# Strassen's seven products for an adjacency multiplication, laid between the products of the weights (Trainium2, float32, one core)

## The chip, the cores and the metric

The kernel runs on one core of a Trainium2 chip. The metric is the device time of one execution in microseconds, of the slowest core; here there is only one. A core has a matrix engine (TensorE, PE in the profile, with its weight loads as PEld), VectorE (DVE), ScalarE (ACT), GpSimd (POOL) and SyncE (SP), which in this kernel only issues transfers. Each engine works through its own stream of instructions in the order in which the program wrote them, and instructions of different engines are tied by waits.

## What is computed

Input `x` is 64 batches of 256 tokens by 512 features, all float32. Two residual layers follow one another; only the first is touched.

```python
# --- layer 0 (adj_preln) ---
h = jnp.maximum(_layernorm(x, axis=-1), 0.0)      # no gain or bias
y = jnp.einsum('nm,bmd->bnd', adj, h)             # adj is 256 x 256, one for all batches
x = x + jnp.einsum('bnd,do->bno', y, weight) + bias
# --- layer 1: layer norm, relu, attention with 8 heads, output product, residual ---
```

## The kernel before

**Groups.** The 64 batches are taken two at a time (`GB = 2`), so there are 32 groups (`NG`). Layer 0 goes through all groups, and leaves two things in DRAM: the new residual and the normed, relued and transposed input of layer 1. Layer 1 then goes through the groups again. Around the border the two are mixed a little: the queries, keys and values of group 0 are made around the weight products of group 31.

**Layer 0 of one group (`layer0`, L702).** First the adjacency product: for each of four feature chunks of 128, and for each batch, two 128x256 matmuls (one for each half of the 256 input tokens) gather into one PSUM bank, 16 matmuls in all (L714), and ScalarE copies each full bank to `yT` (L724). Then the product with the 512x512 weight. It is made by `project` (L456) with Strassen's algorithm in Winograd's form: both operands are cut into 2x2 blocks, some sums of blocks are made beforehand, and seven products take the place of eight. Each product is four 128x256 matmuls (`product`, L448). The seven are seven steps, here called S0 to S6: a11·b11, a12·b21, s2·t2, s3·t3, s1·t1, a22·t4, s4·b22. They accumulate in two long-lived PSUM banks and one short one, and after each of them VectorE adds the bank to a quarter of `x` (L665). The sums t1 to t4 of `yT` are made on GpSimd (L446, `Halves.sums`); those of the weight are made once.

**Layer norms.** `ready` (L678) makes the norm ahead of the adjacency product for a group that is two ahead: for each of four token tiles a statistics instruction and an aggregation on VectorE (L42, L43, "moments"), scale and shift on VectorE and GpSimd (`norm_scales`, L51 to L54), and a relu with that scale and shift on ScalarE (L693). `finished` (L758) makes the norm ahead of layer 1: statistics of each finished quarter of `x` on VectorE (L761, L766), the same scale and shift, a relu on ScalarE (L741), and a 32x32 block transpose on VectorE (`turn`, L747).

**Transfers.** All are issued by SyncE in order: `load` (L295, eight transfers for one group's `x`), `leave_residual` (L751, four for each batch), `leave_hidden` (L756, four for the group).

**What sets the order.** A counter of steps: `run` takes one step of a generator and then calls `tick`, and `after(n, f)` puts `f` at the n-th tick from now. So each engine's order is written out by the program through these delays, and nothing is moved later. A group before has 11 steps (four of the adjacency, seven of the weight); `wait` in `finished` is the number of steps to the relu. Eight PSUM banks are handed out by `bank` and returned by `give`; four buffers of `x` and two of `h` go round.

Of the kernel before, what the change touches and what calls it, by code (L numbers as in the profile page):

```python
# [198 lines left out]
def kernel(  # L199
# [48 lines left out]
    def bank(shape, name, seed=None):  # L248

        i = next(i for i in free_banks if seed is None or whole[i])  # L250
        free_banks.remove(i)
        t = psum.tile(shape, F32, tag=f"bank{i}", name=name)
        bank_of[id(t)] = (i, t)
        if seed is not None:
            nc.scalar.copy(t, seed[:, None, :].to_broadcast(shape))
        return t
# [14 lines left out]
    def tick():  # L271
        clock[0] += 1
        due = sorted((e for e in later if e[0] <= clock[0]), key=lambda e: e[:2])
        later[:] = [e for e in later if e[0] > clock[0]]
        for _, _, fn, args in due:
            fn(*args)
# [14 lines left out]
    def load(g):  # L291
        X[g] = xpool.tile([P, T, D], F32, tag="x", name=f"x_{g}")
        for k in range(GB):
            for i in range(NI):
                nc.sync.dma_start(blocks_of(X[g], i, k), by_block(x[g * GB + k], i))  # L295
# [27 lines left out]
    def turn_adjacency():  # L323
        adj_p = tmp.tile([P, NT, N], F32, tag="u", name="adj_p")
        for u in range(NT):
            nc.vector.tensor_copy(adj_p[:, u, :].rearrange("p (t i b) -> p i t b", i=NI, t=NT),
                                  adj_r[:, u, :].rearrange("p (i t b) -> p i t b", i=NI, t=NT))
        pa = bank([P, NT, N], "pa")
        for t in range(NT):
            for u in range(NT):  # L330
                nc.tensor.transpose(pa[:, t, u * P:(u + 1) * P],
                                    adj_p[:, u, t * P:(t + 1) * P], ident)
        nc.vector.tensor_copy(adjT, pa)  # L333
        give(pa, False)
# [329 lines left out]
    def add(o, ps, u):  # L664
        nc.vector.tensor_tensor(o, ps, u, op=ALU.add)  # L665
# [4 lines left out]
    def split_bias(row):  # L670

        nc.vector.tensor_tensor(row[:, HF:], row[:, HF:], row[:, :HF], op=ALU.subtract)

    def seeded(row, name):
        return tuple(bank([P, 2, N], f"{name}{b}", seed=row[:, h * HF:(h + 1) * HF]) for h, b in enumerate("ac"))


    def ready(g, moments_at, scales_at, relus_at, batches=1):  # L678


        xt = X[g]
        mv = small.tile([P, T, 2], F32, tag="mv", name=f"mv0_{g}")
        n = T // batches
        h = []

        def scales(i):
            h.append(norm_scales(nc, small, mhalf, mv[:, i * n:(i + 1) * n, :], f"0_{g}_{i}"))
            if i == 0:
                H0[g] = act.tile([P, T, D], F32, tag="h", name=f"h_{g}", bufs=2)

        def relu(t):
            rs, nb = h[t // n]
            nc.scalar.activation(H0[g][:, t, :], xt[:, t, :], AF.Relu,  # L693
                                 bias=nb[:, t % n:t % n + 1], scale=rs[:, t % n:t % n + 1])

        for t in range(T):
            after(moments_at[t], moments, nc, small, mv, t, xt[:, t, :], f"0_{g}")
            if (t + 1) % n == 0:
                after(scales_at[t // n], scales, t // n)
            after(relus_at[t], relu, t)  # L700

    def layer0(g):  # L702

        xt, h = X.pop(g), H0.pop(g)

        yT = act.tile([P, DC, GN], F32, tag=f"yT{g % 2}", name=f"yT_{g}")
        halves = Halves(f"y_{g}", [yT[:, :, k * N:(k + 1) * N] for k in range(GB)], g % 2 if g < NG - 1 else 0)
        pss = {}

        def adjacency(d, b):  # L710
            if d not in pss:
                pss[d] = bank([P, GN], f"py_{g}_{d}")
            for k in range(NT):
                nc.tensor.matmul(pss[d][:, b * N:(b + 1) * N], h[:, b * NT + k, d * P:(d + 1) * P],  # L714
                                 adjT[:, k, :], start=(b + k == 0), stop=(k == NT - 1), skip_group_check=True)

        if g == 0:
            for d in range(DC):
                adjacency(d, 0)
        for d in range(DC):  # L720
            for b in range(1 if g == 0 else 0, GB):
                adjacency(d, b)
            ps = pss.pop(d)
            nc.scalar.copy(yT[:, d, :], ps)  # L724
            give(ps)
            halves.sums(nc.gpsimd, ("t1",) if d < 2 else ("t2",), d % 2)
            if d == 3:
                halves.sums(nc.gpsimd, ("t3", "t4"))
            if d == 2:
                seeds = seeded(b0_r, f"w_{g}")  # L730
            yield

        mv = small.tile([P, T, 2], F32, tag="mv", name=f"mv1_{g}")
        st = [small.tile([P, 2, nc.vector.BN_STATS_DIM], F32, tag="st1", name=f"st1_{g}_{t}", bufs=8) for t in range(T)]
        h1 = act.tile([P, T, D], F32, tag="h1", name=f"h1_{g}")
        r = act.tile([P, DC * NI, GB, NT, 32], F32, tag="r", name=f"r_{g}")
        done = []

        def relu(k, rs, nb):
            for t in range(NT):  # L740
                nc.scalar.activation(h1[:, k * NT + t, :], xt[:, k * NT + t, :], AF.Relu,  # L741
                                     bias=nb[:, t:t + 1], scale=rs[:, t:t + 1])

        def turn(k):

            for t in range(NT):
                nc.vector.transpose(r[:, :, k, t, :], h1[:, k * NT + t, :].rearrange("p (j b) -> p j b", b=32))  # L747

        def leave_residual(k):
            for i in range(NI):  # L750
                nc.sync.dma_start(by_block(X1[g][k], i), blocks_of(xt, i, k))  # L751

        def leave_hidden():
            dst = HT[g].rearrange("(j f) d i k n -> i f d j (k n)", f=32)
            for i in range(NI):
                nc.sync.dma_start(dst[i], r[32 * i:32 * i + 32].rearrange("p (d j) k t b -> p d j (k t b)", j=NI))  # L756

        def finished(i, k):  # L758
            o = quarter(xt, i, k)
            for t in range(NT):  # L760
                nc.vector.bn_stats(st[k * NT + t][:, i, :], o[:, t, :])  # L761
            done.append(k)
            if done.count(k) == 2:
                s = slice(k * NT, (k + 1) * NT)
                for t in range(k * NT, (k + 1) * NT):
                    nc.vector.bn_aggr(mv[:, t, :], st[t])  # L766
                rs, nb = norm_scales(nc, small, mhalf, mv[:, s, :], f"1_{g}_{k}")
                wait = 2 if g < NG - 1 else 3
                after(wait, relu, k, rs, nb)
                after(1 if len(done) < 4 else 2, leave_residual, k)  # L770
                after(wait + 1, turn, k)
                if len(done) == 4:
                    after(wait + 2, leave_hidden)

        yield from project(W["0"], halves, True, f"w_{g}", lambda i, k: quarter(xt, i, k), add_to, finished, seeds)


# [12 lines left out]
    def hidden_sums(g, *steps):  # L790

        HH[g] = Halves(f"h_{g}", [H1T[g][:, k] for k in range(GB)], 0 if g else 1)
        for step, n in zip(steps, ("t3", "t1", "t2", "t4")):
            after(step, HH[g].sums, nc.gpsimd, (n,))
# [188 lines left out]
    def run(gen, steps=99):  # L983

        for _ in zip(range(steps), gen):
            tick()
# [1 line left out]

    side = [[] for _ in range(NG)]
    mask_steps, bias_steps = masks(), out_bias()  # L990
    STEPS = 11
    for i, n in enumerate("qkvo"):
        side[2 + 2 * i].append((load_layer1, n))
        side[4 + 4 * i].append((lambda n: weight_sums(nc.gpsimd, L1[n][0], n, [2 + STEPS * j for j in range(4)]), n))
# [4 lines left out]

    ready(0, (0, 0, 2, 2), (0, 2), (1, 1, 3, 3), batches=2)  # L1000
    load(1)
    tick()
    turn_adjacency()
    split_bias(b0_r)
    tick()
    weight_sums(nc.vector, w0_sb, "0", (0, 0, 6, 7))
    load(2)
    tick()
    tick()
    for g in range(NG):  # L1010
        for fn, *args in side[g]:
            fn(*args)

        if g == 0:
            ready(1, (1, 2, 3, 4), (5,), (6, 7, 8, 9))
            ready(2, (8, 8, 10, 11), (12,), (16, 17, 18, 19))
        elif g + 2 < NG:
            ready(g + 2, (1, 4, 7, 8), (9,), (16, 17, 18, 19))
        if g == NG - 2:
            hidden_sums(0, 1, 2, 12, 16)  # L1020
        steps = layer0(g)
        run(steps, 4)
        if g + 3 < NG:
            load(g + 3)
        if g == NG - 3:
            load_hidden(0)
        if g == NG - 1:
            load_hidden(1)
            break
        run(steps)  # L1030
    run(queries_keys(0))
    score(0, 0, 12)
    tick()
    run(steps)
    hidden_sums(1, 1, 2, 6, 7)
# [80 lines left out]
```

## Time and profile before

The median of three runs is 2672.7 us (2672.06 to 2672.92). The profiled execution spans 2669.9 us, with a mean TensorE clock of 0.999.

| what | where in the profile | figure |
|---|---|---|
| adjacency matmuls, 128x256 | L714 on PE, 1024 records | 227.8 us busy |
| their weight loads | L714 on PEld, 1024 records | 195.4 us busy |
| first adjacency matmul, first weight product of group 0 | timeline | 12.07 us, 21.02 us |
| end of group 31's adjacency product, where layer 1's first product begins | timeline | 614.88 us |
| t sums of `yT` on GpSimd | L446, two rows of 96 | 88.0 and 87.2 us busy |
| relu ahead of the adjacency product | L693 on ACT, 128 | 93.9 us, 805 ns each |
| relu ahead of layer 1 | L741 on ACT, 128 | 97.1 us, 807 ns each |
| statistics of finished quarters | L761 on DVE, 256 | 96.4 us, 418 ns each |

A float32 matmul has two records in the profile, as has its weight load. A row of a group reads: line, engine, operation, output and input, shapes, count, then busy time, mean of one, and the idle time of that engine before it with what ended it. A row of the timeline reads: start, busy time, engine, line, operation, output and input, shapes, count of merged records, and in brackets the idle time of the engine before it and the releaser. Ends of matmuls are modelled, so the step from one product's start to the next one's is the measure of its cost.

### The profile page before, as it was taken

How to read it: one execution, taken by the hardware profiler on the slowest of the kernel's cores; microseconds unless marked ns; L12 is line 12 of the kernel's file. 1: busy time of each engine (PE TensorE's matmuls, PEld its weight loads, DVE VectorE, ACT ScalarE, POOL GpSimd, SP SyncE). 2: the span in 40 equal slices, each digit the busy share in tenths (PEclk: the TensorE clock that was granted, in tenths of full speed). 3: DMA queues.
4: the chain of work that ended last, by engine and by line, in shares of the span. 5: the costliest groups of instructions: out<-in, count | busy, mean ns of one | idle time of the engine just before them, and what ended most of it. 6: DMA issues, size and time to landing. Idle time of an engine off the chain costs nothing. (4 is left out here: it accounts for less than half of the span.)

```text
span 2669.9 us, 50186 instructions
## 1 busy us (share of the span) xinstructions
PE 2640.4 (99%) x19332; PEld 2275.8 (85%) x19332; DVE 1849.0 (69%) x4089; ACT 965.3 (36%) x1875; POOL 1793.3 (67%) x1582
## 2 busy tenths in 40 slices
PE   8999999999999999999999999999999999999997
PEld 7888888888888888888888888888888888888885
DVE  6777777774466766666767767667677676676676
ACT  4444445453333333333333333333333333333332
POOL 4454544454787777777777777777777777777775
PEclk9999999999999999999999999999999999999999
DMA  7776666663122211111111111111222111111110
GB/s 185 186 199 169 155 169 166 169 164 78 44 61 58 63 51 48 48 48 48 49 48 48 48 48 48 49 48 49 64 65 62 49 49 48 48 48 49 48 49 33
DMA packets 281059, 210.94 MB, mean 79 GB/s; under 512 B 145904, under 2 KB 212976, under 8 KB 280816
## 3 DMA queue, kind: packets, MB, share of 16 engines
q1 hardware_dynamic: 280352, 207.15, 30.0%
q8 instruction: 155, 2.54, 0.4%
q14 instruction: 88, 0.72, 0.1%
q10 hardware_dynamic: 464, 0.52, 0.1%
HBM read 106.96 MB, written 100.66 MB: 78 GB/s over the span
## 5 line engine op out<-in xcount | busy, mean ns | idle before, releaser
L910 POOL TENSOR_TENSOR a<-a,top 128x1024 f32<-128x1024 f32 x254 | 592.1, 2364 | 488.8 <-DVE a L904 488.8
L904 DVE SCALAR_TENSOR_TENSOR a<-sc,maskT 128x512 f32<-128x512 f32 x512 | 312.1, 682 | 122.0 <-PE sc L898 122.0
L922 POOL TENSOR_TENSOR as<-a 128x512 f32<-128x512 f32 x256 | 318.6, 1277 | 4.0 <-ACT a L915 3.0
L915 ACT ACTIVATE a<-a 128x1024 f32<-128x1024 f32 x256 | 270.9, 1058 | 11.6 <-POOL a L910 10.3
L53 POOL TENSOR_TENSOR rs<-rs,mhalf 128x2 f32<-128x2 f32 (+1 forms) x97 | 78.4, 808 | 268.3 <-DVE nb L52 268.2
L951 DVE RECIPROCAL rest<-rest 128x128 f32<-128x128 f32 x256 | 224.6, 921 | 37.6 <-ACT rest L947 37.6
L898 PE MATMUL sc<-q,k 64*128 64x256 f32 x2048 | 238.4, 382 | 0.0
L938 PE MATMUL pav<-a,v 128*32 128x256 f32 x4096 | 234.0, 379 | 0.0
L898 PEld LDWEIGHTS sc<-q,k 64*128 64x128 f32 x2048 | 194.2, 187 | 44.7 <-issue 26.3
L714 PE MATMUL py<-adjT,h 128*128 128x256 f32 x1024 | 227.8, 381 | 0.9 <-DVE adjT L333 0.9
L714 PEld LDWEIGHTS py<-adjT,h 128*128 128x128 f32 x1024 | 195.4, 191 | 28.4 <-ACT h L693 1.2
L938 PEld LDWEIGHTS pav<-a,v 128*32 128x32 f32 x4096 | 133.5, 110 | 87.9
L741 ACT ACTIVATE h<-x,nb,rs 128x512 f32<-128x512 f32 x128 | 97.1, 807 | 307.2 <-POOL nb L54 307.2
L947 ACT ACTIVATE rest<-pden 128x512 f32<-128x512 f32 x64 | 38.2, 597 | 418.2 <-PE pden L931 418.2
L665 DVE TENSOR_TENSOR k<-k,k 128x128 f32<-128x128 f32 (+1 forms) x300 | 96.1, 353 | 126.1 <-PE k L564 124.0
L446 POOL TENSOR_TENSOR t_y<-yT 128x256 f32<-128x256 f32 (+1 forms) x96 | 88.0, 917 | 44.5 <-ACT yT L724 41.2
L665 DVE TENSOR_TENSOR x<-o,x 128x128 f32<-128x128 f32 (+1 forms) x360 | 111.2, 350 | 3.1
L665 DVE TENSOR_TENSOR q<-q,q 128x128 f32<-128x128 f32 (+1 forms) x300 | 96.1, 353 | 13.8 <-PE q L564 11.7
L665 DVE TENSOR_TENSOR v<-v,v 128x128 f32<-128x128 f32 (+1 forms) x300 | 95.5, 352 | 14.4 <-PE v L564 11.4
L761 DVE BATCH_NORM_STATS2 st<-x 128x6 f32<-128x256 f32 x256 | 96.4, 418 | 4.4
L693 ACT ACTIVATE h<-x,nb,rs 128x512 f32<-128x512 f32 x128 | 93.9, 805 | 10.2 <-POOL nb L54 10.2
L446 POOL TENSOR_TENSOR t_y<-yT,t_y 128x256 f32<-128x256 f32 (+1 forms) x96 | 87.2, 916 | 13.1 <-ACT yT L724 13.0
(4275 smaller groups left out, 6491.5 us busy)
## 6 DMA issues: line engine op xcount, KB each, us to landing
x<-in_x_dram SPq DMA_DIRECT2D x256, 128.0 KB, 3.4
residual<-x SPq DMA_DIRECT2D x256, 128.0 KB, 2.3
hidden<-r SPq DMA_DIRECT2D x128, 256.0 KB, 4.8
h1T<-hidden SPq DMA_DIRECT2D x64, 512.0 KB, 9.6
x<-residual SPq DMA_DIRECT2D x32, 1024.0 KB, 7.5
out_dram<-x SPq DMA_DIRECT2D x62, 512.0 KB, 3.9
w_sb<-in_L_gnn_weight_dram SPq DMA_DIRECT2D x1, 1024.0 KB, 7.3
wq_sb<-in_L_gnn_Wq_dram SPq DMA_DIRECT2D x1, 1024.0 KB, 7.8
```

The costliest lines, as they stand in the source:

```text
L446: eng.tensor_tensor(self.t[n][:, c, :], self.operand(p, c), self.operand(q, c), op=ALU.subtract)
L665: nc.vector.tensor_tensor(o, ps, u, op=ALU.add)
L714: nc.tensor.matmul(pss[d][:, b * N:(b + 1) * N], h[:, b * NT + k, d * P:(d + 1) * P], adjT[:, k, :], start=(b + k == 0), stop=(k == NT - 1 ...
L741: nc.scalar.activation(h1[:, k * NT + t, :], xt[:, k * NT + t, :], AF.Relu, bias=nb[:, t:t + 1], scale=rs[:, t:t + 1])
L761: nc.vector.bn_stats(st[k * NT + t][:, i, :], o[:, t, :])
L898: nc.tensor.matmul(ps[j][:, kt * N:(kt + 1) * N], k[j * HD:(j + 1) * HD, c, kt * P:(kt + 1) * P], q[j * HD:(j + 1) * HD, c, :], start=(kt ...
L904: nc.vector.scalar_tensor_tensor(a[:, j * NT:(j + 1) * NT, :].rearrange("p k n -> p (k n)"), ps[j], SCALE, maskT_f, op0=ALU.mult, op1=ALU.add)
L910: nc.gpsimd.tensor_tensor(a, a, top_b, op=ALU.subtract)
L915: nc.scalar.activation(a, a, AF.Exp)
L922: nc.gpsimd.tensor_tensor(AS[c, b], a4[:, :, 0, :], a4[:, :, 1, :], op=ALU.add)
L938: nc.tensor.matmul(po[f][h * 32:(h + 1) * 32, b * N:(b + 1) * N], v[:, k, h * HD + f * 32:h * HD + f * 32 + 32], A[h // 2, b][:, (h % 2) * ...
L951: nc.vector.reciprocal(rden[:, c * P:(c + 1) * P], den[:, c * P:(c + 1) * P])
```

## The change

The adjacency product of a group is also made by Strassen's algorithm. It isn't a stage of its own any more: its seven products, of four 128x128 matmuls each, are laid between the weight products of the group ahead. The sums that it needs are made on GpSimd: four of adjacency blocks once (`adjacency_sums`, L734), four of the features of each group (`feature_sums`, L745), which follow the relus of that group. The results are put together in `yT` by ScalarE copies and VectorE adds out of PSUM (`adjacency`, L756). Group 0 keeps the old form (`first_adjacency`, L710). Since a group now has seven steps, the delays are set anew: moments, scale and relu of a group are spread over the steps of two groups, and the feature sums over the next. Lines of the changed kernel are given where the text speaks of them.

```diff
-        if g == 0:
-            for d in range(DC):
-                adjacency(d, 0)
         for d in range(DC):
-            for b in range(1 if g == 0 else 0, GB):
-                adjacency(d, b)
...
+    def adjacency_sums():
...
+        for o, p, q in (("t1", block(1, 2), block(1, 1)), ("t2", block(2, 2), AT["t1"]),
+                        ("t3", block(2, 2), block(1, 2)), ("t4", block(2, 1), AT["t2"])):
+            nc.gpsimd.tensor_tensor(AT[o], p, q, op=ALU.subtract)
+
+    def feature_sums(g):
...
+        s1, s2, s4 = (act.tile([P, GB, HF], F32, tag=f"{n}{g % 2}", name=f"{n}_hs_{g}") for n in ("q0", "q1", "k0"))
+        HS[g] = dict(a11=block(1, 1), a12=block(1, 2), a22=block(2, 2), s1=s1, s2=s2, s3=block(2, 1), s4=s4)
+        for o, p, q, op in ((s1, block(2, 1), block(2, 2), ALU.add), (s2, s1, block(1, 1), ALU.subtract),
+                            (block(2, 1), block(1, 1), block(2, 1), ALU.subtract), (s4, block(1, 2), s2, ALU.subtract)):
+            nc.gpsimd.tensor_tensor(o, p, q, op=op)
+
+    def adjacency(g):
...
+        def product(ps, a, b, start=True):
+            for c in range(2):
+                for m in range(GB):
+                    nc.tensor.matmul(ps[:, c, m, :], HS[g][a][:, m, c * P:(c + 1) * P], AT[b],
+                                     start=(start and c + m == 0), stop=True, skip_group_check=True)
...
+        pa = new("a")
+        product(pa, "a11", "b11")
+        nc.scalar.copy(place(0, 0), pa)
+        yield
+        pc = new("c")
+        product(pc, "s3", "t3")
+        nc.scalar.copy(place(1, 1), pc)
+        yield
+        product(pa, "s2", "t2", False)
+        nc.scalar.copy(place(1, 0), pa)
+        yield
+        pb = new("b")
+        product(pb, "a12", "b21")
+        more(pb, 0, 0)
+        give(pb)
+        yield
+        product(pa, "s1", "t1", False)
+        more(pa, 1, 1)
+        yield
+        product(pc, "a22", "t4", False)
+        more(pc, 1, 0)
+        give(pc)
+        yield
+        product(pa, "s4", "b22", False)
+        nc.scalar.copy(place(0, 1), pa)
+        give(pa)
+        after(1, YH[g].sums, nc.gpsimd, ("t1", "t2"))
+        after(3, YH[g].sums, nc.gpsimd, ("t3", "t4"))
+        yield
...
-                wait = 2 if g < NG - 1 else 3
+                wait = 3
...
-    STEPS = 11
+    STEPS = 7
...
     load(1)
+    ready(1, (4, 4, 4, 4), (4,), (5, 5, 6, 6))
+    after(6, feature_sums, 1)
...
-    for g in range(NG):
+    for g in range(NG - 1):
...
-        if g == 0:
-            ready(1, (1, 2, 3, 4), (5,), (6, 7, 8, 9))
-            ready(2, (8, 8, 10, 11), (12,), (16, 17, 18, 19))
-        elif g + 2 < NG:
-            ready(g + 2, (1, 4, 7, 8), (9,), (16, 17, 18, 19))
-        if g == NG - 2:
-            hidden_sums(0, 1, 2, 12, 16)
-        steps = layer0(g)
-        run(steps, 4)
-        if g + 3 < NG:
-            load(g + 3)
+        weighted, turned = layer0(g, seeds), adjacency(g + 1)
+        for i, n in enumerate((0, 0, 0, 1, 1, 2, 3) if g == 0 else (1, 1, 2, 2, 1, 0, 0)):
+            next(weighted)
+            for _ in range(n):
+                next(turned)
+            if i == 5:
+                seeds = seeded(b0_r, f"w_{g + 1}")
+            tick()
+            if i == 3 and g + 3 < NG:
+                load(g + 3)
+
+                ready(g + 3, (2, 2, 3, 3), (3,), (4, 4, 5, 5))
+                after(5, feature_sums, g + 3)
...
+    hidden_sums(0, 1, 1, 2, 2)
+    steps = layer0(NG - 1, seeds)
+    run(steps, 4)
     run(queries_keys(0))
-    score(0, 0, 12)
+    score(0, 0, 6)
```

More of the change, by code (lines that the diff above doesn't have):

```diff
@@ L700, in ready, with begin_y, first_adjacency, part @@
             after(relus_at[t], relu, t)
[L702 to L707, printed above, removed]
+    Y, YH, HS, AT = {}, {}, {}, {}
+    def begin_y(g):
+        yT = Y[g] = act.tile([P, DC, GN], F32, tag=f"yT{g % 2}", name=f"yT_{g}")
+        YH[g] = Halves(f"y_{g}", [yT[:, :, k * N:(k + 1) * N] for k in range(GB)], (g + 1) % 2)
+        return yT
+    def first_adjacency():
+        yT, h = begin_y(0), H0.pop(0)
         pss = {}
-        def adjacency(d, b):
+        def part(d, b):
             if d not in pss:
-                pss[d] = bank([P, GN], f"py_{g}_{d}")
+                pss[d] = bank([P, GN], f"py_{d}")
             for k in range(NT):
@@ L715, in adjacency @@
                                  adjT[:, k, :], start=(b + k == 0), stop=(k == NT - 1), skip_group_check=True)
-        if g == 0:
-            for d in range(DC):
-                adjacency(d, 0)
         for d in range(DC):
-            for b in range(1 if g == 0 else 0, GB):
-                adjacency(d, b)
+            part(d, 0)
+        for d in range(DC):
+            part(d, 1)
             ps = pss.pop(d)
@@ L725, in layer0, with block @@
             give(ps)
-            halves.sums(nc.gpsimd, ("t1",) if d < 2 else ("t2",), d % 2)
+            YH[0].sums(nc.gpsimd, ("t1",) if d < 2 else ("t2",), d % 2)
             if d == 3:
-                halves.sums(nc.gpsimd, ("t3", "t4"))
-            if d == 2:
-                seeds = seeded(b0_r, f"w_{g}")
+                YH[0].sums(nc.gpsimd, ("t3", "t4"))
             yield
+    def adjacency_sums():
+        def block(j, k):
+            return adjT[:, j - 1, (k - 1) * P:k * P]
+        t = act.tile([P, 4, P], F32, tag="t24o", name="adjT_t")
+        AT.update(b11=block(1, 1), b21=block(2, 1), b22=block(2, 2), t1=t[:, 0, :], t2=t[:, 1, :], t3=t[:, 2, :],
+                  t4=t[:, 3, :])
+        for o, p, q in (("t1", block(1, 2), block(1, 1)), ("t2", block(2, 2), AT["t1"]),
+                        ("t3", block(2, 2), block(1, 2)), ("t4", block(2, 1), AT["t2"])):
+            nc.gpsimd.tensor_tensor(AT[o], p, q, op=ALU.subtract)
@@ new lines, in feature_sums, with block @@
+    def feature_sums(g):
+        def block(i, j):
+            return H0[g].rearrange("p (b j) d -> p b j d", b=GB)[:, :, j - 1, (i - 1) * HF:i * HF]
+        s1, s2, s4 = (act.tile([P, GB, HF], F32, tag=f"{n}{g % 2}", name=f"{n}_hs_{g}") for n in ("q0", "q1", "k0"))
[3 more added lines that the diff above has]
+            nc.gpsimd.tensor_tensor(o, p, q, op=op)
@@ new lines, in adjacency, with place, new, more @@
+    def adjacency(g):
+        yT = begin_y(g)
+        H0.pop(g)
+        def place(i, k):
+            return yT[:, 2 * i:2 * i + 2, :].rearrange("p c (b k n) -> p c b k n", b=GB, k=NT)[:, :, :, k, :]
+        def product(ps, a, b, start=True):
[3 more added lines that the diff above has]
+                                     start=(start and c + m == 0), stop=True, skip_group_check=True)
+        def new(n):
+            return bank([P, 2, GB, P], f"py_{g}{n}")
+        def more(ps, i, k):
+            o = place(i, k)
+            add(o, ps, o)
+        pa = new("a")
[27 more added lines that the diff above has]
+        yield
@@ L733, in layer0 @@
+    def layer0(g, seeds):
+        xt, halves = X.pop(g), YH.pop(g)
         mv = small.tile([P, T, 2], F32, tag="mv", name=f"mv1_{g}")
@@ L1001 @@
     load(1)
+    ready(1, (4, 4, 4, 4), (4,), (5, 5, 6, 6))
+    after(6, feature_sums, 1)
     tick()
     turn_adjacency()
+    adjacency_sums()
     split_bias(b0_r)
@@ L1009 @@
     tick()
-    for g in range(NG):
+    steps = first_adjacency()
+    run(steps, 3)
+    seeds = seeded(b0_r, "w_0")
+    run(steps)
+    for g in range(NG - 1):
         for fn, *args in side[g]:
@@ L1014 @@
         if g == 0:
-            ready(1, (1, 2, 3, 4), (5,), (6, 7, 8, 9))
-            ready(2, (8, 8, 10, 11), (12,), (16, 17, 18, 19))
-        elif g + 2 < NG:
-            ready(g + 2, (1, 4, 7, 8), (9,), (16, 17, 18, 19))
-        if g == NG - 2:
-            hidden_sums(0, 1, 2, 12, 16)
-        steps = layer0(g)
-        run(steps, 4)
-        if g + 3 < NG:
-            load(g + 3)
+            ready(2, (1, 1, 2, 2), (2,), (3, 3, 4, 4))
+            after(5, feature_sums, 2)
+        weighted, turned = layer0(g, seeds), adjacency(g + 1)
[10 more added lines that the diff above has]
+                after(5, feature_sums, g + 3)
+        for rest in (weighted, turned):
+            for _ in rest:
+                pass
         if g == NG - 3:
             load_hidden(0)
[L1027 to L1030, printed above, removed]
+    load_hidden(1)
+    hidden_sums(0, 1, 1, 2, 2)
+    steps = layer0(NG - 1, seeds)
+    run(steps, 4)
     run(queries_keys(0))
-    score(0, 0, 12)
+    score(0, 0, 6)
     tick()
```

## The prediction

> **What bounds the kernel now.** I read the page's busy shares first, then the busy time in the stretch of one layer-0 group, then the timeline of that group engine by engine. The page has
>
> ```profile
> PE 2640.4 (99%) x19332; PEld 2275.8 (85%) x19332; DVE 1849.0 (69%) x4089; ACT 965.3 (36%) x1875; POOL 1793.3 (67%) x1582
> ```
>
> so TensorE is the bound overall, and one group of layer 0 (from one adjacency product's start to the next one's; columns after the length: busy PE, PEld, DVE, ACT, POOL) shows no gap on it:
>
> ```profile
> 109.86:128.85 18.99, 18.99 (x89) 16.72 (x88) 14.43 (x39) 8.86 (x14) 9.50 (x13) 1.00 0.65 167
> ```
>
> The timeline around that group's end gives every duration that I need:
>
> ```profile
> 115.71 3.83 SPq L756 DMA_DIRECT2D hidden<-r  x4
> 117.45 2.93 ACT L693 ACTIVATE h<-x,nb,rs 128x512 f32<-128x512 f32 x4
> 119.72 5.34 SPq L295 DMA_DIRECT2D x<-in_x_dram  x8
> 125.40 1.89 PE L453 MATMUL w_5c<-w_sb,t_y 128*128 128x256 f32 x8
> 127.13 1.89 PE L453 MATMUL w_5a<-w_s,yT 128*128 128x256 f32 x8
> 127.23 1.01 POOL L53 TENSOR_TENSOR rs<-rs,mhalf 128x4 f32<-128x4 f32 x1 [6.00 <-DVE nb L52]
> 127.33 0.69 DVE L665 TENSOR_TENSOR x<-w_5c,x 128x512 f32<-128x512 f32 x1
> 128.05 0.75 DVE L761 BATCH_NORM_STATS2 st<-x 128x6 f32<-128x256 f32 x2
> 128.31 0.20 POOL L54 TENSOR_TENSOR nb<-nb,rs 128x4 f32<-128x4 f32 x1
> 128.72 0.33 DVE L766 BATCH_NORM_AGGREGATE mv<-st 128x2 f32<-128x12 f32 x2
> 128.85 7.07 PE L714 MATMUL py<-adjT,h 128*128 128x256 f32 x32
> 129.30 0.68 DVE L665 TENSOR_TENSOR x<-w_5a,x 128x512 f32<-128x512 f32 x1
> 130.41 1.52 ACT L741 ACTIVATE h<-x,nb,rs 128x512 f32<-128x512 f32 x2 [10.03 <-POOL nb L54]
> 131.39 1.31 DVE L747 STREAM_TRANSPOSE r<-h 128x512 f32<-128x512 f32 x2
> 132.62 0.65 DVE L42 BATCH_NORM_STATS2 st<-x 128x6 f32<-128x512 f32 x1
> 133.31 0.18 DVE L43 BATCH_NORM_AGGREGATE mv<-st 128x2 f32<-128x6 f32 x1
> ```
>
> To see: a weight product takes 1.73 us (125.40 to 127.13), seven of them 12.09, the adjacency stage 18.99 - 12.09 = 6.90, or 0.43 for each of 16 matmuls. VectorE starts 0.20 after a product's end, and is held 1.97 us by "add, two statistics, two aggregations, scale, shift" (127.33 to 129.30). Its last such piece falls into the adjacency stage, where it has no adds: that stage is VectorE's and ScalarE's slack.
>
> [...] The trace has just this form in layer 1:
>
> ```profile
> 1411.12 0.38 PE L564 MATMUL v<-spare_w_s,t 128*128 128x128 f32 x2
> ...
> 1414.47 1.89 PE L453 MATMUL o_11a<-wo_sb,oT 128*128 128x256 f32 x8
> ```
>
> 15 matmuls in 3.35 us, 0.223 each: 3% above half of 0.432. [...] a product into a bank waits for the last copy or add from it. [...] 128 KB of x take 3.3 from issue to landing (median), which I use.
>
> **The change part by part, if nothing waits.** TensorE: 16 x 0.432 = 6.90 become 28 x 0.223 = 6.25, saving 0.65 for each of 31 groups, 20 us; a group would take 12.09 + 6.25 = 18.34. GpSimd: four feature sums at 1.27 (L446, 128x512) come in and four t sums become 4 x 1.27: about 14.5 of 18.34. VectorE: three adds at 0.65, 14.4 + 2.0 = 16.4 of 18.34, with its slack stage gone. ScalarE: again four copies. The adjacency sums of the start hide behind loads.
>
> **What the new order makes wait.** Within a group TensorE now runs S0, P1 (a11), S1, s3t3, S2, s2t2, a12b21, S3, s1t1, a22t4, S4, s4b22, S5, S6. Four queues matter:
> - VectorE, in S5 and S6: piece (1,0) 1.97; first pair of moments for the group three ahead; piece (0,1) 1.97; second pair, scale, shift. Only then comes the add of the next group's S0.
> - GpSimd: that scale and shift.
> - ScalarE, next group: copy of P1; two relus L693, which need this scale; two relus ahead of layer 1; copy (1,1); two L693; two more ahead of layer 1; copy (1,0).
> - TensorE: s1t1 goes into the bank which copy (1,0) empties. So the last statistics of a group hold that product in the next.
>
> Lengths: a moment 0.79 (132.62 to 133.31, and 0.10), a pair 1.6. Second pair until GpSimd starts, 1.98 (startup: 12.18 to 14.16). GpSimd 1.31 (127.23, 128.31 + 0.20, ScalarE 0.03 later). Four relus 2.93, so a pair spaced 1.43; a copy 0.5.
>
> *Loop of the engines.* From S5's end: 0.20 + 1.97 + 1.6 + 1.97 + 1.98 + 1.31 = 9.03 until ScalarE has the scale. To the end of copy (1,0): four pairs of relus, two copies and a handoff, 6.86. s1t1 begins, and S5 ends 2 x 0.893 + 1.727 + 0.893 + 1.727 = 6.13 later. Sum 22.0 a group, against 18.99 before.
>
> *Loop with the transfer.* Count from the start M of the first pair of moments. ScalarE has the scale at 1.6 + 1.97 + 1.98 + 1.31 = 6.86. Three pairs and a copy later, at 11.67, it begins the last two relus ahead of layer 1; their transposes begin 0.98 after and take 1.31 (130.41, 131.39): 13.96. SyncE then issues `hidden` of that group and behind it the load of x for the next moments: 4.0 (115.71 to 119.72). The moments need its first four transfers; the fourth was issued at 122.76 and landed some 3.1 later, 6.1 after 119.72. Total 13.96 + 4.0 + 6.1 = 24.1. This is longer than 22.0, so it sets the step: before, the load issued at 119.72 was needed only at 132.62, by the moments in the last rows above. Both relus' wait and the load's wait lie on the path; GpSimd's sums (free from M + 18 to M + 19, when copy (0,1) lets t1 start) do not.
>
> *Start.* Group 1's relus now stand on ScalarE ahead of three copies of group 0's `yT`, and its feature sums ahead of t2 on GpSimd. Walking the queues from the startup timeline (scale of group 1 at 20.8, copies until 26.3, feature sums 24.3 to 29.4) gives S2 of group 0 at 30.9 instead of 24.4, group 1's S0 at 48.5 instead of 40.7, and M for group 1 (moments of group 4) at 72, since t3 of group 1 comes behind the feature sums.
>
> *Sum.* M is reached for groups 1 to 28: 72 + 27 x 24.1 = 722.7. Group 29's S5 ends 19.85 later, then S6 1.73 and group 30 unheld 18.34: 762.6, where it was 614.9. The rest has the same work: +147.7, so 2672.7 + 147.7 = 2820.
>
> **Unknown costs.** The issue and landing behind `hidden`: 4.0 to 4.5 (134.71 to 139.18) and 5.5 to 6.5, so 23.5 to 24.9 a group, 2804 to 2842. The start: 5 us either way. Should transfers land before VectorE asks, the engines' loop is the lower bound, 22.0.
>
> **Rivals.**
> - *The engines' loop alone*, 22.0: 72 + 27 x 22.0 + 39.9 = 705.9, +91, 2764. For it: x lands in 2.8 at best. Against: the issue alone takes 7 of the 10 us.
> - *Queues partly overlap*: if half of the 3.7 us that the engines' loop adds to 18.34 were double counting in my walk, a group would take about 20.2 and the kernel 72 + 27 x 20.2 + 39.9 = 657.3, +42, 2715. Against: each length is a start-to-start distance in the trace, and the order of each queue is fixed.
> - *TensorE stays the bound* (faster): 31 x 0.65 saved, some 8 lost at the start, 2660. For it: no other engine is loaded over 90%. Against: 16.4 of 18.34 on VectorE, with waits on ScalarE in between.
>
> **How the numbers follow.** Transfer loop 0.58, engines' loop 0.24, partial overlap 0.11, TensorE bound 0.07. The predicted time is the first, 2820 us. The range takes in the first two with their unknowns: 2735 to 2855. Faster 0.07, same 0.01, slower 0.92.
>
> **What would show it.** Right: PE gaps in layer 0 ahead of s1t1 released by ScalarE, and ahead of S2 released by VectorE; VectorE idle ahead of moments released by the load of x; ScalarE idle ahead of L693 released by GpSimd's shift; a step of 24 us between groups; layer 1 unchanged. Wrong: steps near 18.3 us, or x landed before its moments.

## The result and the profile after

The changed kernel takes 2841.9 us (median; 2841.0 to 2844.8), where the kernel before takes 2672.4 on the same chip: 1.0636 times as long, with a 95% interval of 1.0618 to 1.0655. The forecast was 2820 with a range of 2735 to 2855.

The page of the changed kernel, its line of busy shares:

```profile
PE 2690.0 (95%) x20076; PEld 2325.1 (82%) x20076; DVE 1917.5 (68%) x4182; ACT 965.4 (34%) x1875; POOL 1940.6 (68%) x1648
```

TensorE has fallen from 99% to 95%, although it is "busy" for 50 us more: its matmuls themselves have become slower, of which more below. The busy time in two stretches of the changed kernel, each from one group's S0 to the next one's (length, then busy PE, PEld, DVE, ACT, POOL, then the granted TensorE clock); the first is group 9, the second group 30, which has no group behind it to wait for:

```profile
246.38:271.00 24.62, 20.49 (x114) 18.29 (x112) 16.74 (x42) 8.88 (x14) 14.22 (x16) 0.93 0.51 132
763.66:782.00 18.34, 18.34 (x113) 16.89 (x112) 12.93 (x32) 6.18 (x10) 6.78 (x9) 1.00 0.76 173
```

Group 30 is the change as it was meant: 18.34 us against 18.99 before, with no gap. Group 9 is what nearly all others are: 24.6 us, of which TensorE idles some 4, and a clock of 0.93. The waits of the whole changed kernel (engine, what waited, what for; us in total, times, longest) name the loop:

```profile
ACT h L693 <- POOL nb L54: 187.4, 32, 10.6
DVE st L42 <- DMA x<-in_x_dram: 66.4, 29, 6.1
POOL q_hs L754 <- ACT h L693: 61.8, 31, 3.5
```

In the kernel before, the first of these lines reads

```profile
ACT h L693 <- POOL nb L54: 10.2, 3, 5.2
```

and the last moments that stood behind their load did so at 17.8 us. The timeline of the changed kernel in group 9, one turn of the loop (start, busy time, engine, line, and in brackets the idle time before it and its end's cause):

```profile
249.24 0.69 DVE L42 BATCH_NORM_STATS2 st<-x 128x6 f32<-128x512 f32 x1 [2.40 <-DMA x<-in_x_dram]
...
255.69 2.69 PE L453 MATMUL w_9a<-w_s,t_y 128*128 128x256 f32 x8 [3.91 <-DVE x L665]
256.28 1.52 ACT L693 ACTIVATE h<-x,nb,rs 128x512 f32<-128x512 f32 x2 [6.42 <-POOL nb L54]
258.18 1.92 PE L767 MATMUL py_10a<-adjT_t,q_hs 128*128 128x128 f32 x8
...
261.00 1.51 ACT L818 ACTIVATE h<-x,nb,rs 128x512 f32<-128x512 f32 x2
261.84 1.42 DVE L824 STREAM_TRANSPOSE r<-h 128x512 f32<-128x512 f32 x2
263.03 1.16 PE L767 MATMUL py_10a<-adjT_t,q_hs 128*128 128x128 f32 x8 [0.21 <-ACT yT L786]
263.29 3.82 SPq L833 DMA_DIRECT2D hidden<-r  x4
267.29 5.31 SPq L295 DMA_DIRECT2D x<-in_x_dram  x8
...
273.51 0.69 DVE L42 BATCH_NORM_STATS2 st<-x 128x6 f32<-128x512 f32 x1 [2.04 <-DMA x<-in_x_dram]
```

From moments (249.24) to the relus that need them (256.28), to the last relus ahead of layer 1 (261.00), to the end of their transposes (263.26), to the stores of `hidden` (263.29), to the load of x behind them on SyncE (267.29), to the next moments that wait for it (273.51): 24.27 us. On the way, TensorE stands 3.91 us ahead of S2, because VectorE's add of S0 is queued behind the moments. The gap ahead of s1·t1 (263.03), which ScalarE's copy (1,0) out of the same bank ends, is 0.21 us.

### The profile page after: what moved, and what is told of

Its sections match the earlier page's. It is cut to its first block, busy times and chain, and to the rows that moved or that the text cites. A ratio compares the mean times of both kernels' runs of the same rounds, so it can differ in the third digit from the quotient of the medians.

```text
span 2839.5 us, 51894 instructions
## 1 busy us (share of the span) xinstructions
PE 2690.0 (95%) x20076; PEld 2325.1 (82%) x20076; DVE 1917.5 (68%) x4182; ACT 965.4 (34%) x1875; POOL 1940.6 (68%) x1648
## 5 line engine op out<-in xcount | busy, mean ns | idle before, releaser
L693 ACT ACTIVATE h<-x,nb,rs 128x512 f32<-128x512 f32 x128 | 97.3, 808 | 187.4 <-POOL nb L54 187.4
L446 POOL TENSOR_TENSOR t_y<-yT 128x512 f32<-128x512 f32 (+1 forms) x65 | 81.5, 1253 | 80.1 <-DVE st L838 78.7
L42 DVE BATCH_NORM_STATS2 st<-x 128x6 f32<-128x512 f32 x128 | 86.7, 677 | 66.4 <-DMA x<-in_x_dram 66.4
L824 DVE STREAM_TRANSPOSE r<-h 128x512 f32<-128x512 f32 x128 | 88.6, 704 | 37.8 <-ACT h L818 37.5
L665 DVE TENSOR_TENSOR v<-v,v 128x128 f32<-128x128 f32 (+1 forms) x300 | 95.5, 352 | 14.5 <-PE v L564 11.5
L818 ACT ACTIVATE h<-x,nb,rs 128x512 f32<-128x512 f32 x128 | 96.4, 802 | 3.9 <-POOL nb L54 3.9
L446 POOL TENSOR_TENSOR t_o<-oT 128x512 f32<-128x512 f32 x64 | 81.8, 1278 | 10.1 <-DVE oT L1046 10.1
```

Source lines behind the costliest of these rows:

```text
L446: eng.tensor_tensor(self.t[n][:, c, :], self.operand(p, c), self.operand(q, c), op=ALU.subtract)
L693: nc.scalar.activation(H0[g][:, t, :], xt[:, t, :], AF.Relu, bias=nb[:, t % n:t % n + 1], scale=rs[:, t % n:t % n + 1])
```

## The experiments

All are made from the changed kernel by moving instructions; the arithmetic is that of the changed kernel in every run, except that two of them do extra products which nobody reads. A "step" is the distance from one group's S0 to the next one's.

**Cutting the loops one at a time.** *The load early* puts the load of x ahead of the stores of `hidden`, and so cuts the loop with the transfer.

```diff
-            if i == 3 and g + 3 < NG:
+            if i == 2 and g + 3 < NG:
                 load(g + 3)
+            if i == 3 and g + 3 < NG:
                 ready(g + 3, (2, 2, 3, 3), (3,), (4, 4, 5, 5))
```

> Only the place of the load of x changes: it is issued one step earlier, ahead of the stores of hidden. My theory (the step of 24.6 us per group is set by a loop through the last transposes, the stores of hidden, the load of x, the statistics and the relus): the loop loses the 4.0 us of the stores' issue, so the shorter loop of the engines takes over, 22.0 to 22.4 us per group; 27 x (24.65 - 22.2) = 66 us less, 2776 us. Rival (the engines' amount of work or the small matmuls set the step, the waits are a symptom): unchanged, 2842 us within 5.

Measured: 2801.9 us, 1.0479 [1.0459, 1.0499] times the kernel before. VectorE's moments no longer wait for x, so the transfer is off the loop. But it brings 40 us where 66 were expected: 15 of the 30 steps are 23.8 rather than 22.0. The busy time in two steps of this kernel shows why:

```profile
241.22:265.05 23.83, 20.50 (x114) 18.38 (x113) 16.65 (x42) 8.89 (x14) 14.26 (x16) 0.93 0.53 137
546.23:568.58 22.35, 18.84 (x113) 16.89 (x112) 16.98 (x43) 8.90 (x14) 13.17 (x15) 1.00 0.56 146
```

Where the clock is 1.00 a step is 22.35; where it is 0.93 the same products take 1.66 us more. That is followed up below.

*The relus later* leaves the load where it was, and sets the relus L693 behind the copy (1,0), which cuts the engines' loop.

```diff
-                ready(g + 3, (2, 2, 3, 3), (3,), (4, 4, 5, 5))
-                after(5, feature_sums, g + 3)
+                ready(g + 3, (2, 2, 3, 3), (3,), (6, 6, 7, 7))
+                after(7, feature_sums, g + 3)
```

> Only the four relus ahead of the adjacency product (and the feature sums behind them) move, two steps later, so that ScalarE does the relus ahead of layer 1 and the copies first. My theory: ScalarE no longer carries the late scale to the product s1t1, but VectorE's queue still has the last transposes behind the statistics and adds, which end some 11.9 us after the first moments begin; with 4.0 + 6.1 for stores and load that is 22.0 us per group, 2773 us. If ScalarE alone were the cause and the load were not: 19.8, 2711 us. Rival (amount of work): unchanged, 2842 us.

Measured: 2831.5 us, 1.0592 [1.0575, 1.0610]: a miss. ScalarE's relus ahead of layer 1 do come early now, but their transposes don't. The timeline of this kernel in group 10:

```profile
267.74 0.69 DVE L42 BATCH_NORM_STATS2 st<-x 128x6 f32<-128x512 f32 x1 [2.35 <-DMA x<-in_x_dram]
...
274.19 3.48 PE L453 MATMUL w_10a<-w_s,t_y 128*128 128x256 f32 x8 [4.34 <-DVE x L665]
...
278.56 1.06 PE L767 MATMUL py_11b<-adjT,h 128*128 128x128 f32 x8
...
280.08 0.69 DVE L665 TENSOR_TENSOR yT<-py_11b,yT 128x512 f32<-128x512 f32 x1 [1.69 <-PE py_11b L767]
280.69 1.30 DVE L824 STREAM_TRANSPOSE r<-h 128x512 f32<-128x512 f32 x2
282.01 3.83 SPq L833 DMA_DIRECT2D hidden<-r  x4
286.02 3.48 SPq L295 DMA_DIRECT2D x<-in_x_dram  x4
...
292.44 0.69 DVE L42 BATCH_NORM_STATS2 st<-x 128x6 f32<-128x512 f32 x1 [2.45 <-DMA x<-in_x_dram]
```

On VectorE the last transposes stand behind the add of a12·b21, which waits for TensorE, which waited 4.34 us for VectorE's add of S0, which stood behind the moments. So the same loop closes through VectorE and TensorE in 24.7 us. The edit took one branch away where there were two of nearly equal length. Part of that length is the lowered clock, to which the text comes below: S2 and s2·t2 take 4.37 us here (274.19 to 278.56), and 2.62 at full clock, so at full clock this loop would take about 23.0 (an estimate from these two figures).

*Both edits together:*

> Both edits together. My theory: neither the load nor ScalarE holds the step any more; what stays is that the add of the next group's first weight product stands on VectorE behind 7.5 us of statistics and holds the third weight product: 19.8 us per group, 27 x 4.85 = 131 us less, 2711 us, still slower than before. Rival (amount of work): unchanged, 2842 us, since every engine does the same work.

Measured: 2729.7 us, 1.0214 [1.0197, 1.0231]. Most steps are 20.45 to 20.48 rather than 19.8. TensorE has one gap left in each, in this kernel's timeline:

```profile
345.28 1.97 PE L453 MATMUL w_15a<-w_s,t_y 128*128 128x256 f32 x8 [1.90 <-DVE x L665]
```

What follows from the three: the same work in another order is 112 us faster than the change as it was made. It is the waits, not the amount of work; and both loops must be cut, as one alone leaves 2802 or 2832.

**The clock.** In the changed kernel TensorE's granted clock is not 1.00 after its gap. Busy time of the changed kernel from 258.18 to 259.88, during the product s2·t2 right after the S2 of the timeline above:

```profile
258.18:259.88 1.70, 1.70 (x9) 1.70 (x8) 1.34 (x3) 1.70 (x4) 1.70 (x2) 0.50 0.00 0
```

Half the clock, and the product takes 1.70 where one of the same size takes 0.89 at full clock (248.10 to 248.99 in the same group). To test that idling is the cause, two kernels fill TensorE's gaps with products of the adjacency with itself, in front of the waiting instruction. *The changed kernel kept busy:*

```diff
+    def keep_busy(n):
+        i = free_banks[0]
+        was = whole[i]
+        ps = bank([P, GN], "idle")
+        for _ in range(n):
+            nc.tensor.matmul(ps[:, 0:P], AT["b11"], AT["b11"], start=True, stop=True, skip_group_check=True)
+        give(ps, was)
...
+            if i == 2 and 0 < g < NG - 3:
+                keep_busy(14)
             next(weighted)
```

> The changed kernel with 14 products of 128x128 (the adjacency with itself, read by nobody, 14 x 0.223 = 3.1 us) put in TensorE's queue just ahead of S2, where it stands idle for 3.7 to 3.9 us. They hide in the gap and take no result's place. Theory, that the 0.55 us by which the step was above the forecast is the lowered clock of the matmuls behind the gap (0.86 to 0.93 granted in those groups): the clock in the windows goes back to about 1.0, S2 takes 1.9 us instead of 2.7 to 3.7, the step 24.1, the whole 2842 - 27 x 0.55 = 2827. Rival, that the clock falls for another reason or its slow matmuls are not on the loop: 2842, or more where the products outlast the gap.

Measured: 2833.3 us, 1.0604 [1.0587, 1.0620]: 8.6 us less, where the theory wanted 14.9. Not all of the 8.6 is the loop's. In the profiled executions the loop, from group 1's moments to group 28's, is 4.6 us shorter, and another 3.2 us are missing behind the queries of group 1, in layer 1, which the edit doesn't touch. What the products do to the loop: in six of its 27 turns in the changed kernel the last transposes ended 15.1 to 15.5 us after the moments rather than 14.0, because the add ahead of them on VectorE waited for slow matmuls; with the products it is one. The clock is 1.00 over 23 of the 28 steps from group 2 on, and in the other five a gap took it down again (a step of 25.62 at 0.93). Still a turn of the loop, from moments to moments, takes 24.48 us on average, against 24.65 without the products. So in this kernel the lowered clock costs some 0.2 us a turn; the waits make the rest. *The early load, both gaps filled:*

```diff
+            if i == 2 and 0 < g < NG - 3:
+                keep_busy(7)
             next(weighted)
+            if i == 3 and 0 < g < NG - 3:
+                keep_busy(6)
```

> The kernel with the early load alone runs most groups in 23.83 us at a granted clock of 0.93 and six of them in 22.3 us at 1.00; my engines' loop was 22.0. Here 7 and 6 products of 128x128 that nobody reads (1.56 and 1.34 us by 0.223 each) stand in TensorE's queue in its two gaps, 1.8 us ahead of S2 and 1.7 us ahead of s1t1. Theory, that the lowered clock comes from the idling and lies on the engines' loop: clock 1.00 in every group, 22.4 a group, 2802 - 19 x 1.5 = 2773. Rival, that the clock falls by itself, or that the products stand in the way (they are as long as the gaps): 2802 or more.

Measured: 2778.2 us, 1.0394 [1.0377, 1.0411], 24 us less than the early load alone, although TensorE has more to do. Busy time in one step of this kernel:

```profile
231.49:253.65 22.16, 21.64 (x139) 19.95 (x138) 16.64 (x42) 8.88 (x14) 14.23 (x16) 1.00 0.59 159
```

The clock is 1.00, and 17 steps are 22.16 or 22.17. So the lowered clock comes from the idling here, lies on the engines' loop, which this kernel is left with, and costs 1.7 us a step there (23.83 to 22.16); and the engines' loop of the forecast, 22.0, is right to 0.2.

**Taking out the rest of the order.** *Spread:* the load stays early, the moments are spread over three weight steps, so that no add stands behind two pairs, the relus come behind both copies, and the feature sums and two of the products move.

```diff
-        after(1, YH[g].sums, nc.gpsimd, ("t1", "t2"))
-        after(3, YH[g].sums, nc.gpsimd, ("t3", "t4"))
+        after(1, YH[g].sums, nc.gpsimd, ("t1", "t2", "t3"))
+        after(3, YH[g].sums, nc.gpsimd, ("t4",))
...
-    ready(1, (4, 4, 4, 4), (4,), (5, 5, 6, 6))
-    after(6, feature_sums, 1)
+    ready(1, (4, 4, 4, 4), (4,), (8, 8, 8, 8))
+    after(9, feature_sums, 1)
...
-        for i, n in enumerate((0, 0, 0, 1, 1, 2, 3) if g == 0 else (1, 1, 2, 2, 1, 0, 0)):
+        for i, n in enumerate((0, 0, 0, 1, 1, 2, 3) if g == 0 else (1, 0, 2, 2, 2, 0, 0)):
...
+            if i == 2 and g + 3 < NG:
+                load(g + 3)
...
-                ready(g + 3, (2, 2, 3, 3), (3,), (4, 4, 5, 5))
-                after(5, feature_sums, g + 3)
+                ready(g + 3, (4, 4, 6, 7), (7,), (8, 8, 9, 9))
+                after(9, feature_sums, g + 3)
```

> The same products and sums in an order worked out from the loops: load one step earlier; moments of the group behind VectorE's adds of the next group's steps S0, S2 and S3 and scale there, relus in S4 and S5, feature sums after them; the product s3t3 one step later, the sum t3 two steps earlier; at the start the relus of group 1 behind the copies of group 0. My theory: VectorE has 16.4 us of work in 18.34 and gets it done between the adds, so TensorE is the bound again, 18.34 to 18.7 us per group, and the start loses 1 to 3 us in place of 8: 2656 to 2675 us. Rival (amount of work): some 24 us per group, 2820 us or more; the engines cannot do this work faster in another order.

Measured: 2673.8 us, 1.0007 [0.9998, 1.0015]: as the kernel before, at the upper end of what was expected. A step is 18.85. Nearly all of the half microsecond over 18.34 lies at two products, for which an operand or a bank gets ready at the very end, so that their first weight load waits. The timeline of this kernel in group 20:

```profile
412.45 0.97 PEld L767 LDWEIGHTS py_21c<-adjT_t,h 128*128 128x128 f32 x8 [0.24 <-POOL h L754]
...
417.13 0.97 PEld L767 LDWEIGHTS py_21a<-adjT_t,q_hs 128*128 128x128 f32 x8 [0.19 <-ACT yT L786]
```

On PE itself these show as no idle time at all, and yet they cost: s3·t3 starts 0.07 late, at 412.45, at the same time as its first weight load, and takes 1.00 to the next product's start instead of 0.89; with s1·t1 it is 0.17 and 0.10. *Just in time* (the diff is against the spread order) moves both producers forward: feature sums ahead of the norm's scale, relus ahead of layer 1 behind the copies (1,1) and (1,0).

```diff
-                wait = 3
+                wait = 3 if g == NG - 1 else 5 if len(done) < 4 else 4
...
-            ready(2, (1, 1, 2, 2), (2,), (3, 3, 4, 4))
-            after(5, feature_sums, 2)
+            ready(2, (2, 2, 3, 4), (4,), (5, 5, 6, 6))
+            after(7, feature_sums, 2)
...
-        for i, n in enumerate((0, 0, 0, 1, 1, 2, 3) if g == 0 else (1, 0, 2, 2, 2, 0, 0)):
+        for i, n in enumerate((0, 0, 0, 1, 2, 2, 2) if g == 0 else (1, 0, 2, 2, 2, 0, 0)):
+            if i == 5 and 0 < g < NG - 2:
+                feature_sums(g + 2)
...
-                ready(g + 3, (4, 4, 6, 7), (7,), (8, 8, 9, 9))
-                after(9, feature_sums, g + 3)
+                ready(g + 3, (4, 4, 5, 6), (6,), (7, 7, 7, 7))
```

> On top of the spread order: both reluctant places of that run are taken out. The relus ahead of layer 1 (L818) go behind the copies of (1,1) and (1,0) on ScalarE (waits 5 and 4 steps instead of 3), the four relus ahead of the adjacency go into ScalarE's idle stretch ahead of the copy of (0,1), the sums of the features stand ahead of the norm's scale on GpSimd, and at the start the moments of group 2 come later and the products of group 1 are spread over three steps. In the spread order a group took 18.85 us, 0.5 above 18.34, of it 0.18 at s3t3 behind the sums of the features and 0.27 at s1t1 behind the copy of (1,0), and group 1 began at 45.1 us. My theory, that what is left are such handovers and nothing of the amount of work: 18.4 a group, group 1 from about 43: 2674 - 27 x 0.45 - 2 = 2660, below the kernel before. Rival, that the half microsecond lies in TensorE's own changes between operands: 2670 to 2674.

Measured: 2680.4 us, 1.0032 [1.0020, 1.0044]: 0.3% slower than the kernel before, a miss. The two waits are gone, and group 1 begins at 40.9 us, but two others came. In group 20 of this kernel's timeline the add of S0 now stands behind the statistics of S6's quarter (the scale at 410.44), and S2 behind that add:

```profile
410.44 0.78 DVE L51 TENSOR_SCALAR rs<-mv 128x2 f32<-128x2 f32 x1
...
411.20 0.68 DVE L665 TENSOR_TENSOR x<-w_20a,x 128x512 f32<-128x512 f32 x1
412.03 1.97 PE L453 MATMUL w_20a<-w_s,t_y 128*128 128x256 f32 x8 [0.16 <-DVE x L665]
```

The other: S2 of group 1 waited 4.5 us for t1 and t2, which stood behind group 2's feature sums on GpSimd. *Statistics late* (the diff is against just in time) is that kernel with the statistics of the last quarter put behind the next group's first add, and group 2's feature sums put two steps earlier.

```diff
+            late = len(done) == 4 and g < NG - 1
+            if late:
+                after(2, statistics, i, k, True, 2)
+            else:
+                statistics(i, k, done.count(k) == 2, 3 if g == NG - 1 else 5)
...
-            ready(2, (2, 2, 3, 4), (4,), (5, 5, 6, 6))
-            after(7, feature_sums, 2)
+            ready(2, (2, 2, 3, 4), (4,), (5, 5, 5, 5))
+            after(5, feature_sums, 2)
```

> e5 lost on two counts that its trace names: S2 waited 0.33 us in each group for VectorE's add of S0, which stood behind the statistics of the last weight step (410.4 to 411.2), and S2 of group 1 waited 4.5 us for the sums t1 and t2 behind the sums of the features of group 2 on GpSimd. Here the statistics of the last quarter come one step later, behind the add of S0, and the features of group 2 stand two steps earlier. If these are the causes: about 18.4 us a group plus the turned weights of layer 1 now and then, layer 1 from about 600 us instead of 620, total 2655 to 2660, below the kernel before. Rival, that VectorE (18.0 us busy of 18.86) is now what bounds a group, whatever its order: 18.8 a group, 2670.

Measured: 2654.8 us (2653.9 to 2656.5), 0.9938 [0.9924, 0.9951] of the kernel before, and the slowest run (2656.5) is well under the fastest of that kernel (2670.4). Busy time in a step of this kernel:

```profile
375.49:393.83 18.34, 18.34 (x113) 16.91 (x112) 17.72 (x42) 9.11 (x14) 14.10 (x17) 1.00 0.64 172
```

A step is 18.34 in 26 of the 29 groups from 2 to 30; the other three carry side work for layer 1 on TensorE. Between 200 and 600 us of that run TensorE is busy for 400.00. VectorE is busy for 17.7 of these 18.3 us, so its load doesn't bound the group; in the kernels before this one its order did. *Spread and start* was the control: the spread order with only the second of the relus L818 one step later and the new start.

```diff
-                wait = 3
+                wait = 3 if len(done) < 4 or g == NG - 1 else 4
...
-            ready(2, (1, 1, 2, 2), (2,), (3, 3, 4, 4))
+            ready(2, (2, 2, 3, 4), (4,), (5, 5, 5, 5))
...
-        for i, n in enumerate((0, 0, 0, 1, 1, 2, 3) if g == 0 else (1, 0, 2, 2, 2, 0, 0)):
+        for i, n in enumerate((0, 0, 0, 1, 2, 2, 2) if g == 0 else (1, 0, 2, 2, 2, 0, 0)):
```

> The spread order (2673.8) with two edits only: the last two relus ahead of layer 1 one step later, behind the copies of (1,1) and (1,0), and the start of e7 (products of group 1 over three steps, moments of group 2 later, its features two steps earlier). The copy (1,0) no longer holds s1t1 (0.27 us a group), group 1 begins at 41 instead of 45 and S2 of group 1 waits under 1 us: 2674 - 27 x 0.27 - 3.5 = 2663. If VectorE's load is the bound: 2670; if the start is all there is to win: 2670.

Measured: 2667.1 us, 0.9981 [0.9974, 0.9988]. Steps are 18.57 to 18.61: the copy's wait is gone (0.27), the feature sums' wait is left (0.24 over 18.34). It came 4 us above what was expected.

## Why the prediction was right, and where it was off

The direction, the loop that sets the step and the range held; the sum was 22 us short: 169.6 us more (of span) where 147.7 were forecast.

- **The work if nothing waits, 18.34 a group: right.** Group 30 of the changed kernel and the groups of the statistics-late kernel that carry no side work take 18.34. So do the loads: VectorE 16.7 for 16.4, GpSimd 14.2 for 14.5, ScalarE 8.9 as before.
- **The loop with the transfer: the right loop.** From M, the start of the moments: the relus at 7.04 (forecast 6.86), the last relus ahead of layer 1 at 11.76 (11.67), end of the transposes 14.02 (13.96), stores to load 4.0 (4.0), load to moments 6.22 (6.1), all in group 9. (A transfer of x in the kernel before takes 2.5 us from issue to landing at the least and 3.4 in the median, where the forecast has 2.8 and 3.3.) The waits that were to show it are in the lines above: VectorE's for x, ScalarE's for the shift, and on TensorE the 3.91 us ahead of S2; the one ahead of s1·t1 is there too, but 0.21 us only. The margin was thinner than the forecast had it: the engines' loop, priced at 22.0 against 24.1, takes 23.8 with its slow matmuls, as the early load shows.
- **The step of 24.1: the mis-sized term.** Over the 27 turns it is (741.91 - 76.26) / 27 = 24.65, and 27 x 0.55 = 14.9 us of the miss. Of all 27, the transposes end at 14.32 on average (0.36 more than 13.96), and from the load's issue to the moments it takes 6.27 (0.17 more than 6.1). About 0.27 of the 0.36 comes from the six turns of 15.1 to 15.5. There the forecast's path was incomplete: it let the last transposes follow ScalarE's relus alone, while on VectorE they also stand behind the add of a12·b21, and so behind TensorE, whose matmuls after a gap I had priced at full clock. With TensorE kept busy the transposes end at 14.08. The 0.17, transfers that land later than 6.1 in some turns (5.84 to 6.91), I did not pursue.
- **The start.** S2 of group 0 was to come at 30.9; it began at 30.1, stood still for its second sum and went on at 31.0. Group 1's S0 at 48.6 (forecast 48.5) was right. M for group 1 came at 76.3 instead of 72, 4.3 us of the miss. The wait for t3 that the forecast named is there, 5.40 us ahead of S3 of group 1. S3, s1·t1 and a22·t4 behind it take 6.45 us (63.20 to 69.65) instead of 3.51 at full clock: 2.9 us by the same omission. Where the other 1.4 went was not traced.
- **"Layer 1 unchanged": 2.5 us off.** 0.7 us lie between S0 of group 31 and the queries of group 1 (61.66, where before it is 60.92 from the same point). From there to the end it is 1995.8 against 1994.1, and the other kernels of this study, none of which touches it, have 1992.5 to 1996.6: no more than scatter.
- **The rivals.** The engines' loop alone (22.0, 2764) is what is left with the load early and TensorE kept busy: steps of 22.16. "Half of it double counting" (20.2) was refuted by that. "TensorE stays the bound, 2660" is not this kernel, but it is this work: in another order it takes 2654.8. My argument against it, 16.4 of 18.34 on VectorE with waits in between, was right about the waits and would have been wrong about the load.

In short, the change did bring its 0.65 us of TensorE time a group, and lost 6.3 us by where the delays put four moments, the relus and the load. Put elsewhere, the same instructions keep the 0.65: (596.2 - 41.2) / 30 = 18.50 a group in the fastest kernel against (614.9 - 40.7) / 30 = 19.14 before, side work included, 19 us of gain over the 30 steps, of which 17 arrive.

## What to carry to other kernels

When work is laid between the steps of another stage, follow each queue once round: from a bank that must be emptied, through the engine that empties it, to what stands ahead of that copy or add, and to what that waits for, transfers included. A loop through several groups sets the step though no engine is full, and cutting one of two branches of like length wins little (40 us and 10 here, 112 together), so look for the second before you cut the first. Where a trace shows the granted clock at half behind a gap on TensorE, as here behind 1.88 us in the early-load kernel and 3.91 in the changed one, price the matmuls behind the gap at that clock (1.70 us instead of 0.89 for a product of four 128x128) for as long as the trace shows it (3.41 or 6.83 us in the two cases of the next section), and check whether that stretch is on the loop: it cost 1.7 us a step with the early load, and some 0.2 a turn in the changed kernel, where mostly other waits ended later.

## What the runs showed of the hardware

I had not expected that gaps this short take TensorE's clock down. In the profile of the early-load kernel the granted clock fell behind a gap of 1.88 us ahead of s1·t1 in the 23.8 us steps (0.93 over the step). In the 22.35 us steps of the same kernel, with gaps of 1.79 and 1.72, it reads 1.00 over the whole step, and so it does in the ten steps of the kernel with both edits, between 213.53 and 461.24, whose gap ahead of S2 is 1.88 to 1.90. Three stretches of the early-load kernel's profile:

```profile
252.75:256.16 3.41, 1.53 (x10) 1.10 (x9) 2.70 (x5) 2.63 (x5) 2.51 (x3) 1.00 0.04 11
256.16:259.58 3.42, 3.42 (x15) 3.22 (x15) 1.46 (x3) 0.00 (x0) 2.50 (x3) 0.50 0.98 252
556.54:559.95 3.41, 2.36 (x14) 1.80 (x12) 2.70 (x5) 3.41 (x6) 1.19 (x1) 1.00 0.00 0
```

The first holds a whole gap of 1.88, and TensorE is busy for 1.53 of its 3.41 us; the next 3.42, the second line, run at half clock. The third holds 1.05 us of a gap of 1.72, and TensorE is busy for 2.36; the clock is 1.00 there and in the rest of that step (546.23 to 568.58). So about 1.9 us of idling was enough in one of these kernels and left the clock up in another; what decides between them was not shown. How long the half clock lasted, in the changed kernel at the gaps of 3.71 us in group 8 (226.55 to 230.26) and 3.91 in group 9 (251.78 to 255.69):

```profile
229.47:236.30 6.83, 6.04 (x20) 5.36 (x21) 4.09 (x8) 5.45 (x9) 4.20 (x5) 0.50 0.51 135
236.30:239.71 3.41, 3.41 (x25) 3.20 (x24) 2.51 (x5) 1.25 (x3) 3.33 (x4) 1.00 0.35 120
256.78:260.19 3.41, 3.41 (x15) 3.06 (x14) 2.00 (x5) 3.41 (x6) 3.15 (x3) 0.50 0.02 5
260.19:263.61 3.42, 3.21 (x21) 2.65 (x21) 2.75 (x5) 2.79 (x5) 2.35 (x2) 1.00 0.00 0
```

In group 8 it is 0.50 for 6.83 us, in group 9 for 3.41, and then 1.00 again. In group 9's stretch the product of four 128x128 matmuls from 258.18 to 259.88 took 1.70 us instead of 0.89.
